# Attention stage of a hybrid block: key projection from mean-free inputs, first batch loaded in four parts, two score-maximum transposes made one

## Chip, cores, metric

The kernel runs on one core of a Trainium2 chip, as one launch. The metric is the device time in microseconds (us) of that core. Before the change three runs gave a median of 1651.34 us (1651.06 to 1651.93).

## What is computed

Eight batches of 512 tokens with 256 features pass through three blocks: a sparse attention with 16 heads of 16 features, a gated linear attention with a feed-forward part, and block-routed feed-forward layers with residuals. Only the first block is touched by the change. Each block is applied to a normalized input. The reference of the attention is

```python
scale = 1.0 / jnp.sqrt(jnp.asarray(DH, dtype=x.dtype))
q = _split_heads(x @ Wq + bq)
k = _split_heads(x @ Wk + bk)
v = _split_heads(x @ Wv + bv)
scores = jnp.einsum('bhqd,bhkd->bhqk', q, k) * scale
sparsity = scores.max(axis=-1) - scores.mean(axis=-1)
_, top_idx = jax.lax.top_k(sparsity, U)          # U = 307 of 512 queries
q_sel = jnp.take_along_axis(q, top_idx[..., None], axis=2)
scores_sel = jnp.einsum('bhud,bhkd->bhuk', q_sel, k) * scale
attn = jax.nn.softmax(scores_sel, axis=-1)
out_sel = jnp.einsum('bhuk,bhkd->bhud', attn, v)
out = jnp.zeros_like(q).at[bi, hi, top_idx].set(out_sel)
return out.transpose(0, 2, 1, 3).reshape(b, l, D) @ Wo + bo
```

If the mean over the keys is taken off every key of a head, the mean of a query's scores is zero. The maximum of the mean-free scores is then the sparsity itself, and the softmax does not change, since each query's scores are shifted by one constant.

## The kernel before

The whole program is one function with SBUF tiles for everything. All matrices are float32. The work on the engines is issued in an order written out in loops; a scheduler then fixes each engine's order, and each engine executes its instructions strictly in that order.

**Loads.** The input of batch 0 (`xres[:, 0]`, 512 KB) is one load on SP's queue (line 48). ACT's queue issues the padded `wq` and `wk` (512 KB each) and `wv` (256 KB, line 77). POOL copies the used columns out of the padded `wq` and `wk` (line 133). SP then issues the bias columns `bq` and `bk`, four small loads each (line 143), the broadcast rows `bo` and `bv` (line 89), and batch 1 (line 162), which is held back until the statistics of batch 0 exist. Batches 2 to 7 are loaded by the same line at later steps.

**Selectors.** `head_of` (POOL, lines 166 to 174) marks the first 16 of each 32 partitions. `own`, `one`, `kept` and `bq_own` (DVE, lines 175 to 187) are made from it and from `ident`. Each of two groups `m` of eight heads fills 128 partitions, 16 for each head, and its q and k are kept in two versions `e` = 0, 1, which hold the even and the odd heads, so that each block of 32 partitions has one head and 16 spare rows.

**front(b)** prepares a batch in pieces (a generator, one piece at each `yield`): DVE (or ACT) normalizes to `xn`; POOL adds `bo` to the residual `xres` (line 286); PE transposes `xn` in two halves (line 295) and ACT copies each to `xnT`, with the sum over the tokens as a by-product (`xsum`, line 298); then for two groups `m` PE projects queries and keys (`q_ps`, `k_ps`, line 316), ACT or DVE write the two versions of q (lines 329, 334), ACT those of k (line 367); then the values (`v_ps`, lines 376 and 385). Between the first q and the first k there is a piece that makes the mean key: eight PE instructions with one column each (`km_ps`, line 344), and four small DVE instructions (lines 350 to 355), which turn it into the bias `kb` of line 367. That bias takes the mean key off each key.

**Steps.** A list of 128 steps (batch, m, e, k) drives the rest. In step n, `max_one` computes four score tiles of 128x512 (PE, line 422) and reduces each to its row maxima (DVE, line 425, to `mx`). Sixteen steps later (`LAG`) `exp_one` computes four transposed score tiles of the older step (PE, line 433), ACT takes the exponential (line 437), and one step after that `weigh` multiplies with the values (PE, line 442). `take` copies the sums out (ACT, line 452), sends a part to `den` (line 454), and POOL puts the halves together (lines 457 to 460). In the first 14 steps (`LEAD`) the pieces of `front(0)` and `front(1)` run between the maxima; later one piece of `front(b + 2)` follows each step. PSUM has three banks for the tag "e" (`bank`), four for "m" (`bank_m`) and one for `acc`; with maxima and exponentials in one step, line 433 uses the first and line 422 the second, and the pieces of `front` also use `bank_m`.

**Placing maxima.** After the last of four steps of a group and version, `place_maxima(b, m, e)` transposes the 16 columns of maxima (PE, line 401), negates them (ACT, line 403) and sends them with eight small DMAs on SP's queue: four into spare rows of the older q (line 406), so that line 433's scores have the maximum taken off, and four into `neg` (line 411). From `neg`, after the last maximum, DVE selects the top queries (lines 467 to 474, 26 rounds), and PE and DVE scale the outputs (lines 617 to 630).

**After the attention** (line 636 on) come the output projection and the other two blocks, which the change leaves as they are.

Of the kernel before, what the change touches and what calls it, by code (L numbers as in the profile page):

```python
# [10 lines left out]
F32 = mybir.dt.float32  # L11
# [27 lines left out]
def block_kernel(ctx: ExitStack, tc: tile.TileContext, t: dict, out: bass.AP):  # L39
# [8 lines left out]
    nc.sync.dma_start(out=xres[:, 0], in_=x_in[:, 0])  # L48

    ident = keep.tile([P, P], F32, name="ident")  # L50
    make_identity(nc, ident)
    eps = keep.tile([P, 1], F32, name="eps")
    nc.gpsimd.memset(eps, LN_EPS)
# [45 lines left out]
    with ExitStack() as outer:  # L99
# [21 lines left out]
        mx = a_out.tile([P, NB, NG, 4 * 4], F32, name="mx")  # L121
# [3 lines left out]
        with ExitStack() as inner:  # L125
# [3 lines left out]

            def load_heads(name, src, eng):  # L130
                wp = load_chunked(a1, name + "_pad", src, eng)
                w = a1.tile([P, NC2, D], F32, name=name)
                nc.gpsimd.tensor_copy(
                    w.rearrange("p c (h d) -> p (c h) d", d=DH),
                    wp.rearrange("p c (h q) -> p (c h) q", q=32)[:, :, 0:DH],
                )
                return w

            def load_head_column(name, src, eng):
                w = a1.tile([P, NC2], F32, name=name)  # L140
                for g in range(NG):
                    r = 64 * (g % 2)
                    eng.dma_start(
                        out=w[r : r + 64, g // 2 : g // 2 + 1],
                        in_=src.rearrange("(j q) g -> j q g", q=32)[:, 0:DH, g : g + 1],
# [13 lines left out]
            def load_after(b, part):  # L159
# [5 lines left out]
            head_of = a1.tile([P, 4], F32, name="head_of")  # L165
            nc.gpsimd.memset(head_of, 1.0)
            nc.gpsimd.affine_select(
                out=head_of, in_=head_of, compare_op=ALU.is_ge, fill=0.0,
                base=0, pattern=[[-32, 4]], channel_multiplier=1,
            )  # L170
            nc.gpsimd.affine_select(
                out=head_of, in_=head_of, compare_op=ALU.is_ge, fill=0.0,
                base=DH - 1, pattern=[[32, 4]], channel_multiplier=-1,
            )
# [11 lines left out]
            for e in range(2):  # L186
                nc.vector.tensor_scalar(bq_own[:, e, :], bq, own[:, e : e + 1], None, ALU.mult)

# [80 lines left out]
            fronts = {}  # L269

            def front(b, pick, alone):
# [3 lines left out]
                for k in range(4):  # L275
# [5 lines left out]
                    else:  # L281
                        nc.vector.tensor_scalar(
                            xn[:, k, :], xres[:, b, k, :], mean, rs, ALU.subtract, ALU.mult
                        )

                nc.gpsimd.tensor_tensor(
                    xres[:, b], xres[:, b],
                    bo.unsqueeze(1).to_broadcast([P, 4, D]), ALU.add,
                )
                xnT = a2.tile([P, NC2, L], F32, tag="xnT", name=f"xnT{b}")  # L290
                xsum = a2.tile([P, NC2], F32, tag="xsum", name=f"xsum{b}")
                for c in range(NC2):
# [7 lines left out]
                    )  # L300
                    yield
# [10 lines left out]
                fronts[b] = (qs, ks, va)  # L312
                kb = a2.tile([P, 2, NC2], F32, tag="kb", name=f"kb{b}")

                def project(ps, w, m, c):
                    nc.tensor.matmul(  # L316
                        ps, w[:, c, bass.ts(m, P)], xnT[:, c, :],
# [3 lines left out]
                for m in range(NC2):  # L321
                    ps = pick(f"q_ps{b}")
                    for c in range(NC2):
                        project(ps, wq, m, c)
# [14 lines left out]
                    if m == 0:  # L339

                        pm = pick(f"km_ps{b}")
                        for mm in range(NC2):
                            for c in range(NC2):
                                nc.tensor.matmul(
                                    pm[:, mm : mm + 1], wk[:, c, bass.ts(mm, P)],
                                    xsum[:, c : c + 1],
                                    start=(c == 0), stop=(c == NC2 - 1),
                                )
                        km = a2.tile([P, NC2], F32, tag="km", name=f"km{b}")
                        nc.vector.scalar_tensor_tensor(  # L350
# [920 lines left out]
```

## Time and profile before

| | |
|---|---|
| median of 3 runs | 1651.34 us |
| profiled execution, its own time | 1653.55 us |
| span of the trace of that execution | 1651.8 us |
| mean granted TensorE clock | 0.988 of full speed |
| busy: PE, DVE, ACT, POOL | 1599.0, 969.4, 671.7, 334.3 us |
| DMA moved | 27.58 MB, mean 17 GB/s |
| line 422 (maxima's scores) / line 433 (exponentials' scores) on PE | 298.9 / 294.3 us busy |
| line 425 (row maxima) on DVE | 329.0 us busy, 684 ns each |
| line 437 (exponentials) on ACT | 276.1 us busy, 599 ns each |

The busy time of an engine is the union of its instructions' spans. PE is shown busy whenever a matmul is under way, so a high share says that it had work, not that the work was as fast as it could be. The trace can also be read as a chain: from the last instruction back to what released each one. An engine that is not on this chain has time to spare at that point.

### The profile page before, as it was taken

To read this page: it belongs to the slowest core of one execution; us is meant where nothing else is said; L and a number is where in the kernel's file an instruction comes from. 1 tells how busy PE (TensorE), PEld (TensorE's weight loads), DVE (VectorE), ACT (ScalarE), POOL (GpSimd) and SP (SyncE) were. 2 spreads that over 40 slices of the span, in tenths; PEclk is the share of its full clock that TensorE was granted. 3 is DMA by queue.
4 is the path that set the end of the run, shared out by engine and by line. 5 is a ranking of instruction groups with operands and counts; after the bars stand their busy time and mean duration, and the time that the engine had idled before them with its cause. 6 is when DMAs were issued, how large, how long until landed. Compare 5 with 4: busy or idle time off the path is not lost.

```text
span 1651.8 us, 19680 instructions
## 1 busy us (share of the span) xinstructions
PE 1599.0 (97%) x7378; PEld 820.1 (50%) x7378; DVE 969.4 (59%) x2015; ACT 671.7 (41%) x1208; POOL 334.3 (20%) x381
## 2 busy tenths in 40 slices
PE   7999999999999969999989999999999999999999
PEld 3323223333233237655564556555555556766666
DVE  6978776676667786447672666277355633344342
ACT  2366666665656814252346123622521352121010
POOL 3111111010000102114342442154223421000000
PEclk9999999999999979999999999999999999999999
DMA  3100000000000051010000001000000010011100
GB/s 109 40 2 3 2 2 3 2 2 3 2 3 3 2 165 26 3 37 13 1 1 0 1 1 27 0 0 1 0 1 1 0 26 1 20 33 35 43 26 26
DMA packets 24276, 27.58 MB, mean 17 GB/s; under 512 B 6229, under 2 KB 20725, under 8 KB 24181
## 3 DMA queue, kind: packets, MB, share of 16 engines
q1 hardware_dynamic: 23108, 24.75, 5.2%
q10 hardware_dynamic: 1072, 1.57, 0.3%
q8 instruction: 58, 0.95, 0.2%
q14 instruction: 38, 0.30, 0.1%
HBM read 21.20 MB, written 4.33 MB: 15 GB/s over the span
## 4 chain that ended last, share of the span: by engine, by line
PE 77%; DVE 14%; ACT 3%; POOL 3%; issue 1%; DMA 1%; SPq 0%; ACTq 0%; POOLq 0%; DVEq 0%
PE y_ps L889 16%; PE h_ps L909 11%; PE s L433 8%; PE s L422 8%; PE swi_ps L936 7%; PE proj_ps L1019 7%; PE av L442 7%; DVE pr L1052 2%; DVE pr L1042 2%; PE ao_ps L775 2%; PE q_ps L316 2%; PE gla_y L1144 2%; DVE mx L425 2%; PE v_ps L376 2%; PE k_ps L316 2%; POOL o L1069 1%
## 5 line engine op out<-in xcount | busy, mean ns | idle before, releaser
L425 DVE TENSOR_REDUCE mx<-s 128x1 f32<-128x512 f32 x512 | 329.0, 684 | 129.8 <-PE s L433 83.0
L437 ACT ACTIVATE e<-s 128x512 f32<-128x512 f32 x512 | 276.1, 599 | 179.0 <-PE s L433 103.5
L422 PE MATMUL s<-k,q 32*128 32x512 f32 x1024 | 298.9, 641 | 3.2 <-ACT k L367 2.5
L433 PE MATMUL s<-q,k 32*128 32x512 f32 x1024 | 294.3, 638 | 0.4 <-DVE mx L425 0.3
L889 PE MATMUL y_ps<-w,h 128*128 128x256 f32 x1024 | 232.9, 383 | 2.9 <-DVE h L918 2.9
L909 PE MATMUL h_ps<-xnT,w 128*128 128x512 f32 x512 | 229.8, 597 | 4.1 <-ACT h L917 4.1
L889 PEld LDWEIGHTS y_ps<-w,h 128*128 128x128 f32 x1024 | 194.1, 192 | 41.0 <-issue 10.8
L909 PEld LDWEIGHTS h_ps<-xnT,w 128*128 128x128 f32 x512 | 95.5, 191 | 113.8 <-issue 107.1
L442 PE MATMUL av<-e,va 128*32 128x512 f32 (+1 forms) x1120 | 141.9, 568 | 3.8 <-ACT e L437 2.4
L918 DVE TENSOR_TENSOR h<-h,mk 128x512 f32<-128x512 f32 x128 | 97.6, 774 | 78.9 <-ACT h L917 70.0
L917 ACT ACTIVATE h<-h_ps,b 128x512 f32<-128x512 f32 x96 | 65.6, 684 | 178.1 <-PE h_ps L909 178.0
L422 PEld LDWEIGHTS s<-k,q 32*128 32x128 f32 x1024 | 89.5, 184 | 86.0 <-DVE mx L425 56.1
L433 PEld LDWEIGHTS s<-q,k 32*128 32x128 f32 x1024 | 88.1, 183 | 80.8 <-ACT e L437 53.8
L894 DVE TENSOR_TENSOR xres<-xres,y_ps 128x512 f32<-128x512 f32 x48 | 32.8, 683 | 162.2 <-PE y_ps L889 125.0
L936 PE MATMUL swi_ps<-zT,w_gate 128*128 128x512 f32 x256 | 122.7, 599 | 4.8 <-DVE h L945 4.8
L936 PE MATMUL swi_ps<-zT,w_up 128*128 128x512 f32 x256 | 121.2, 594 | 0.0
L1019 PE MATMUL proj_ps<-q_w,rT 128*128 128x512 f32 x256 | 118.3, 601 | 0.0
L889 PE MATMUL y_ps<-w_down,h 128*128 128x256 f32 x512 | 116.8, 380 | 0.0
L889 PEld LDWEIGHTS y_ps<-w_down,h 128*128 128x128 f32 x512 | 95.7, 190 | 20.0 <-issue 8.5
L942 ACT ACTIVATE h<-swi_ps 128x512 f32<-128x512 f32 x64 | 38.2, 596 | 156.7 <-PE swi_ps L936 156.6
L1069 POOL TENSOR_TENSOR o<-o,pr 128x512 f32<-128x512 f32 (+2 forms) x56 | 80.9, 1444 | 58.9 <-DVE pr L1052 56.9
L797 POOL TENSOR_TENSOR xres<-xres,b 128x512 f32<-128x512 f32 x32 | 40.1, 1271 | 240.0 <-ACT row L737 217.7
(191 smaller groups left out, 1713.9 us busy)
## 6 DMA issues: line engine op xcount, KB each, us to landing
mk<-md SPq DMA_DIRECT2D x32, 256.0 KB
xres<-in_L_attn_a_x SPq DMA_DIRECT2D x8, 512.0 KB
out<-xres SPq DMA_DIRECT2D x16, 256.0 KB
q<-negT SPq DMA_DIRECT2D x128, 2.0 KB
neg<-negT SPq DMA_DIRECT2D x128, 2.0 KB
w<-in_f_w1T SPq DMA_DIRECT2D x1, 1024.0 KB
w<-in_f_w2T SPq DMA_DIRECT2D x1, 1024.0 KB
w_gate<-in_b_w_gateT SPq DMA_DIRECT2D x1, 1024.0 KB
```

The source lines that it names most:

```text
L316: nc.tensor.matmul(ps, w[:, c, bass.ts(m, P)], xnT[:, c, :], start=(c == 0), stop=(c == NC2 - 1),)
L422: nc.tensor.matmul(s, qs[e][rows, m, bass.ts(k, P)], ks[e][rows, m, :], start=True, stop=True)
L425: nc.vector.tensor_reduce(mx[:, b, 2 * e + m, r : r + 1], s, AX.X, ALU.max)
L433: nc.tensor.matmul(s, ks[e][rows, m, bass.ts(kt, P)], qs[e][rows, m, :], start=True, stop=True)
L437: nc.scalar.activation(ex, s, AF.Exp, scale=1.0 / DH**0.5)
L442: nc.tensor.matmul(av[32 * j : 32 * j + 32, queries], va[:, 8 * kt + 4 * m + j, e, :], es[j][:, queries], start=(kt == 0), stop=(kt == 3 a ...
L889: nc.tensor.matmul(y[0][:, bass.ts(i, D)], h[f][:, bass.ts(2 * u + i, P)], w[:, f, :], start=(f == 0), stop=(f == NF - 1),)
L909: nc.tensor.matmul(ps, w1[:, c, bass.ts(f, P)], xT[g][:, c, :], start=(c == 0), stop=(c == NC2 - 1),)
L918: nc.vector.tensor_tensor(hf, hf, mk[g][:, f, :], ALU.mult)
L936: nc.tensor.matmul(ps, w[:, c, bass.ts(f, P)], zT[g][:, c, :], start=(c == 0), stop=(c == NC2 - 1),)
L1019: nc.tensor.matmul(ps, rT[b // G4][:, c, bass.ts(b % G4, P)], q_w[:, c, m], start=(c == 0), stop=(c == NC2 - 1),)
L1069: nc.gpsimd.tensor_tensor(dst, dst, src, ALU.add)
```

## The change

Parts that only move are cut. The selectors `head_of` now stand ahead of the weight loads on POOL; the tile that takes a padded weight is a buffer of the tag `k1` (three buffers, otherwise the odd keys); `bq` and `bk` come in two loads each instead of four.

```diff
-    nc.sync.dma_start(out=xres[:, 0], in_=x_in[:, 0])
+    for k in range(4):
+        (nc.scalar if k % 2 else nc.sync).dma_start(out=xres[:, 0, k], in_=x_in[:, 0, k])
...
-        mx = a_out.tile([P, NB, NG, 4 * 4], F32, name="mx")
+        mx = a_out.tile([P, NB, NC2, 2, 4 * 4], F32, name="mx")
...
+            def load_heads(name, src, eng):
+                wp = a2.tile([P, NC2, L], F32, tag="k1", name=name + "_pad", bufs=3)
...
+                for r in range(2):
+                    eng.dma_start(
+                        out=w[64 * r : 64 * r + 64, :],
+                        in_=src.rearrange("(j q) g -> j q g", q=32)[:, 0:DH, r::2],
+                    )
...
+            bk_kept = a1.tile([P, 2, NC2], F32, name="bk_kept")
+            nc.gpsimd.tensor_tensor(bk, bk, bk, ALU.subtract)
+            for e in range(2):
+                nc.vector.tensor_scalar(
+                    bk_kept[:, e, :], bk, kept[:, e : e + 1], one[:, e : e + 1],
+                    ALU.mult, ALU.add,
+                )
...
-                nc.gpsimd.tensor_tensor(
-                    xres[:, b], xres[:, b],
-                    bo.unsqueeze(1).to_broadcast([P, 4, D]), ALU.add,
-                )
+                if not alone:
+                    add_bias(b)
                 xnT = a2.tile([P, NC2, L], F32, tag="xnT", name=f"xnT{b}")
+                xcT = a2.tile([P, NC2, L], F32, tag="xcT", name=f"xcT{b}", bufs=1)
...
                     nc.scalar.activation(
                         xnT[:, c, :], ps, AF.Identity, accum_out=xsum[:, c : c + 1]
                     )
+                    mean = xmean[:, c : c + 1]
+                    if b == 0:
+                        nc.vector.tensor_scalar(mean, xsum[:, c : c + 1], -1.0 / L, None, ALU.mult)
+                        nc.vector.tensor_scalar(xcT[:, c, :], ps, mean, None, ALU.add)
+                    else:
+                        nc.scalar.mul(mean, xsum[:, c : c + 1], -1.0 / L)
+                        nc.scalar.activation(xcT[:, c, :], ps, AF.Identity, bias=mean)
                     yield
...
-                    if m == 0:
-                        pm = pick(f"km_ps{b}")
-                        for mm in range(NC2):
-                            for c in range(NC2):
-                                nc.tensor.matmul(
-                                    pm[:, mm : mm + 1], wk[:, c, bass.ts(mm, P)],
-                                    xsum[:, c : c + 1],
...
-                        nc.vector.scalar_tensor_tensor(
-                            km, pm[:, 0:NC2], 1.0 / L, bk, ALU.mult, ALU.add
-                        )
-                        nc.vector.tensor_tensor(km, bk, km, ALU.subtract)
-                        for e in range(2):
-                            nc.vector.tensor_scalar(
-                                kb[:, e, :], km, kept[:, e : e + 1], one[:, e : e + 1],
...
-                        project(ps, wk, m, c)
+                        project(ps, wk, xcT, m, c)
...
-                            bias=kb[:, e, m : m + 1], scale=kept[:, e : e + 1],
+                            bias=bk_kept[:, e, m : m + 1], scale=kept[:, e : e + 1],
...
-            def place_maxima(b, m, e):
+            def place_maxima(b, m, es):
+                n = 16 * len(es)
+                pt = bank_m(f"mxT_ps{b}")[0:n, 0:P]
+                nc.tensor.transpose(
+                    pt, mx[:, b, m].rearrange("p e n -> p (e n)")[:, 16 * es[0] : 16 * es[0] + n],
+                    ident,
+                )
+                negT = a2.tile([32, P], F32, tag="negT", name=f"negT{b}")
+                nc.scalar.mul(negT[0:n, :], pt, -1.0)
...
-            for _ in range(7):
+            for _ in range(6):
                 next(first)
...
-                1: batch_stats([1], None, maximum_of(0)),
+                1: batch_stats([1], lambda: fronts[0][3][0:1, 1, 0:1], maximum_of(0)),
...
                 if ahead is not None and ahead[3] == 3:
-                    full.append((n + 2, ahead[0:3]))
+                    b, m, e = ahead[0:3]
+                    if b == NB - 1 and m == 1:
+                        full.append((n + 2, (b, m, (e,))))
+                    elif e == 1:
+                        full.append((n + 2, (b, m, (0, 1))))
...
+                    if n == 9:
+                        nc.gpsimd.tensor_copy(bo_late[0:1, 0:1], maximum_of(n))
+                        nc.gpsimd.tensor_copy(bo_late, bo)
+                        for b in range(2):
+                            add_bias(b)
...
-                    while done < 23 * (n + 1) // LEAD:
+                    while done < 22 * (n + 1) // LEAD:
```

In words: the token mean is taken off the transposed input itself (`xcT`), and the keys are projected from that instead of from `xnT`. The mean-key piece and its PSUM bank go, and the bias of line 367 becomes a constant. `xcT` is written by DVE for batch 0 and by ACT for the others, from the same PSUM bank as `xnT`. `add_bias` is the addition of `bo` to the residual, from a late copy of `bo`; for batches 0 and 1 it moves to step 9. The statistics of batch 1 wait for `xcT` of batch 0. The maxima of both versions of a group are transposed together after the second; only the last group of the last batch is still done in two halves. The DMAs that place the maxima are as many as before.

## The prediction

> **What bounds the kernel now.** I read busy time by stage first, then the chain of waits from the start to the last maximum, then single microseconds. The stages (from:to, length, busy PE, PEld, DVE, ACT, POOL with counts, granted clock, DMA share, GB/s):
>
> ```profile
> 0.00:19.90 19.90, 8.18 (x24) 4.38 (x24) 8.01 (x38) 4.92 (x11) 7.71 (x23) 1.00 0.47 145
> 19.90:71.10 51.20, 50.26 (x215) 21.28 (x215) 46.51 (x99) 14.96 (x29) 10.36 (x18) 0.97 0.20 63
> 206.00:472.00 266.00, 266.00 (x1728) 82.55 (x1728) 185.16 (x312) 162.87 (x316) 29.54 (x27) 1.00 0.01 3
> 541.00:612.00 71.00, 54.31 (x319) 18.25 (x320) 56.12 (x118) 36.67 (x71) 8.69 (x13) 0.86 0.28 83
> 612.00:1651.80 1039.80, 1019.66 (x3749) 630.74 (x3747) 522.46 (x1178) 325.20 (x545) 255.18 (x263) 0.99 0.05 14
> ```
>
> There are four regimes. Up to 19.9 us no engine is half busy: waits rule. From 19.9 to 71.1 maxima run alone and DVE is busy 46.51 of 51.20. From 71 to 541 exponentials run beside maxima and PE has no gap (266.00 of 266.00 in the middle). From 541 the top queries hold DVE. After 612 come stages that the change does not touch: in the built programs their instructions stand in the same order on every engine, so they can only move as a whole.
>
> The start and two pieces of the middle, as the chain of waits has them (start, length, what), and the rows that hold the start up:
>
> ```profile
> 0.79 5.43 DMA xres<-in_L_attn_a_x
> 8.75 1.26 DVE xn L282 x4
> 10.01 5.46 DMA xres<-in_L_attn_a_x
> 15.49 0.75 DVE ln_st L221 x2
> 19.10 0.79 ACT k L367
> 19.93 1.15 PE s L422 x8
> ...
> 147.38 0.21 PE mxT_ps L401
> ...
> 153.47 0.98 PE km_ps L344 x8
> ```
> ```profile
> 16.84 0.36 DVE L187 TENSOR_SCALAR bq_own<-bq,own 128x2 f32<-128x2 f32 x2
> ...
> 18.71 0.48 DVE L355 TENSOR_SCALAR kb<-km,kept,one 128x2 f32<-128x2 f32 x2
> ```
>
> Batch 0 lands at 6.22, but the chain then runs through batch 1's load (issued 10.01, landed 15.47): DVE's order puts batch 1's statistics ahead of the selectors, of `bq_own` and of the mean-key instructions, so q and k of batch 0 wait for another batch. The first score starts at 19.93.
>
> **The change part by part.**
>
> *(1) Start.* Four loads on two queues put all of batch 0 ahead of `wq`; before, 512 KB of each came together. Four loads from 4 to 7 us ran at 381 to 387 GB/s, and x and `wq` landed at 6.22 and 6.0, so x alone is down about 512 KB / 385 GB/s = 1.4 us earlier, near 4.9. But in the new order ACT issues `wk` only when a part of x is in, and `wv` only when `bq` is, and its table load (1.28) and the root come behind these. I put xn at 8.0 instead of 8.66, transposes done and `xnT` at 10.6 instead of 11.25 and the first q matmul at 10.75 instead of 11.44. q took 11.44 to 14.80, so it ends at 14.1; k follows with its 1.96, ending 16.1 (`xcT` is two DVE pieces of about 0.8, the row of q on line 334, done by 13). Batch 1's load no longer stands behind eight small bias loads but four; SP reaches it near 7, not 10.01, and with its 5.46 it lands by 12.5. Its statistics (DVE 15.49 to 17.75 before, with selectors among them; about 1.9 alone) are over by 15, its root by 15.4. That is before k ends, so k is written at 16.2 to 17.0 and the first score starts at 17.0: 3.0 earlier. Bounds: 1.5, if batch 1 lands at 14.5 and is again last; 4.5, if xn starts 1.4 earlier and k runs at the pace of later k pieces (1.06 each, against 1.96).
>
> The Trainium skill, page "DMA: Bandwidth & Descriptors", section "Issuing engines are not separate DMA queues", says that loads issued by several engines share the same 16 DMA engines and that only issue time is saved. By that rule the second queue would be worth one or two issues of about 0.45, some 0.5 to 1 us here, and this term would be near its lower bound.
>
> *(2) Clock.* Between k (17.4) and the first score PE idled 2.52 us, and then the granted clock fell (columns as above, the clock third from the end; it is back at 24.7):
>
> ```profile
> 21.00:22.00 1.00, 1.00 (x6) 0.45 (x2) 0.83 (x2) 0.00 (x0) 0.16 (x1) 0.55 0.00 0
> 22.00:23.00 1.00, 1.00 (x6) 0.05 (x4) 0.95 (x3) 0.75 (x2) 0.02 (x1) 0.50 0.00 0
> ```
>
> In my sum PE idles 0.9 there. DVE waited 0.86 (24.01 to 24.87) for slow scores, so 0.86 is the most that full clock gives. I take 0.8, lower bound 0.
>
> The skill's page "TensorE: Matmul & The Clock Gate", section "What's actually happening", lets the clock fall after an idle window of about 3.4 us, free-running. The idle gap here was 2.52 us, so by that rule alone there would have been no fall; the row decides.
>
> *(3) Lead, 20 to 71.* DVE loses batch 1's four mean-key instructions: 0.14 + 0.16 + 0.48 = 0.78. PE loses one piece of 0.98, beside DVE's work. Four POOL copies gate batch 1's statistics (0.17 each) during a wait. Adding `bo` to batches 0 and 1 moves to step 9; POOL works there 2.35 us for each, before `spread` and long before `outC` needs it (busy 10.36 of 51.20), and next to maxima at an unchanged 0.6 each. ACT's extra pieces for batch 1 fit (14.96 of 51.20). Gain 0.8, bounds 0 and 1.8 (the piece counts too where two fall in a step).
>
> *(4) Mean-key piece.* Fronts 2 to 7 run beside exponentials, where PE has no gap: 6 x 0.98 = 5.9. Bounds 4.9 (one of the six ends in a wait for something else) and 5.9.
>
> *(5) Transposes of maxima.* 32 become 17. Before, 3 fall in the lead and 29 later; after, 1 and 16. So 13 x 0.21 = 2.7, if a transpose of 32 columns costs as one of 16 (the moved side is 128 wide in both); bounds 2.0 and 2.7. SP issues the same DMAs, 16 in a row instead of 8; at some 0.6 each the older half gets its row four steps later, at step 9 + 2 of a group whose exponentials start at step 16: five steps of 4.1 us spare. The last group is split as before, so the wait from the last maximum to the top queries stays.
>
> *(6) Price on ACT.* Each of 12 transposed halves of fronts 2 to 7 gets a mean (about 0.2, the size of the accumulator row) and an `xcT` (0.60) on ACT, and holds its PSUM bank until then (one such half before, in order of time: start, length, engine and line, the idle time before it in brackets):
>
> ```profile
> 207.07 0.66 PE L295 MATMUL xnT_ps<-ident,xn 128*128 128x128 f32 x4
> 208.17 0.60 ACT L298 ACTIVATE xnT<-xnT_ps 128x512 f32<-128x512 f32 x1
> 208.65 0.21 ACT L298 ACTIVATION_READ_ACCUMULATOR xnT<-xnT_ps 128x1 f32 x1
> 208.82 1.08 ACT L437 ACTIVATE e<-s 128x512 f32<-128x512 f32 x2
> 211.21 1.09 ACT L437 ACTIVATE e<-s 128x512 f32<-128x512 f32 x2 [1.31 <-PE s L433]
> ```
>
> ACT idles 1.31 before the next exponentials, which covers 0.8. But the new ACT order is `xnT`, mean, one exponential, `xcT`, one exponential: mean to 209.1, exponential to 209.65, `xcT` to 210.2. The third score of the next half step, which PE starts at 209.97, takes the bank that `xcT` reads: 0.25 late. That is 12 x 0.25 = 3.0. Bounds: 0, if the four scores in different row groups absorb it; 9.6, if the whole 0.8 shows each time. I take 3.0, the worked row. Queued behind that score are the fourth score, then the next half step; DVE, with 1.3 idle in these steps, follows.
>
> *The sum.* 3.0 + 0.8 + 0.8 + 5.9 + 2.7 - 3.0 = 10.2. Against the profiled span: 1651.8 - 10.2 = 1641.6, and 1643.35 with the 1.75 that lies around it (1653.55). The median of the runs, 1651.34, is 2.2 under that execution, so I predict 1641.1.
>
> **Rivals.** *A, the start gives nothing and ACT takes all.* Term 1 at 1.5, 2 and 3 at 0, 6 at 9.6: 1.5 + 4.9 + 2.7 - 9.6 = -0.5, no change, 1651.8. For it speaks that `xcT` shares a bank with maxima; against it the 1.31 of ACT's idle time.
>
> *B, no price on ACT, and a good start.* 4.5 + 0.86 + 1.8 + 5.9 + 2.7 = 15.8: 1635.5. For it: PE packs four scores, and a late third one may cost nothing.
>
> *C, slower: the held bank.* One place: line 422's third score after each transposed half. If `xcT` there waits for both exponentials of the half step, as `xnT` did when scores came first, the score is late by mean, 1.08 of exponentials and `xcT`: 0.2 + 1.08 + 0.6 less the 0.25 that ACT was ahead, about 1.6. 12 x 1.6 = 19.2 against gains of 13.2: 1657.3. It decides from 13.2 / 12 = 1.1 us a piece. Against it: the built order has only one exponential between.
>
> *D, the change doesn't do what it says at the start:* batch 1's statistics still end last and the score starts at 19.9. Then 0.8 + 5.9 + 2.7 - 3.0 = 6.4: 1644.9. For it: ACT's root for batch 1 still stands before k.
>
> **How the numbers follow.** The forecast, 1641.1 with its own range of 1637 to 1645, gets 0.50; D 0.19, B 0.18, A 0.06, C 0.07. The range leaves out A and C and the end of B: 1635 to 1648, which takes in half of the price bound as well. A measurement of this kernel tells about 0.2%, 3.3 us, from no change. Faster by more: 0.50 + 0.19 + 0.18 = 0.87; same 0.06 (A); slower 0.07 (C).
>
> **What would show it.** The first score at 17 (start right), above 19 (D). The clock at 1.00 from 20 to 25. Period of a batch between transposes: 67.37 before (274.51 to 341.87), 67.37 - 0.98 - 2 x 0.21 = 65.97 without a price, 66.5 with mine, 69 in C, where PE would show idle time on line 432 released by `xcT`. The stage after the last maximum should keep its length of 1111 (540.34 to the end); clock dips in it that fall elsewhere would be outside this sum, and would make it wrong by a few us.

## The result, and the profile after

The changed kernel took 1650.8 us (median of 14 runs, 1648.84 to 1653.82), the kernel before on the same chips 1651.47 (14 runs, 1650.05 to 1652.73). The ratio is 0.9997 with a 95% interval of 0.9989 to 1.0005: no measurable change, where 10 us had been predicted. The profiled execution took 1650.2 us by its own time, with a span of 1648.5 and a mean granted clock of 0.988.

Busy time by stage in the changed kernel (from:to, length, busy PE, PEld, DVE, ACT, POOL with counts, granted clock, DMA share, GB/s), cut where its own first score, first exponentials and last maximum stand:

```profile
0.00:17.77 17.77, 6.95 (x17) 3.41 (x17) 9.24 (x40) 4.96 (x11) 6.12 (x27) 1.00 0.57 163
17.77:69.00 51.23, 50.33 (x213) 21.45 (x215) 47.48 (x98) 18.76 (x36) 13.20 (x21) 1.00 0.20 63
206.00:472.00 266.00, 265.83 (x1680) 81.36 (x1676) 182.62 (x296) 166.79 (x325) 29.49 (x27) 1.00 0.01 3
539.00:610.00 71.00, 56.80 (x323) 19.39 (x324) 55.85 (x118) 36.67 (x71) 8.78 (x13) 0.83 0.27 84
610.00:1648.50 1038.50, 1018.64 (x3746) 630.80 (x3744) 522.35 (x1178) 325.22 (x545) 255.48 (x263) 0.99 0.05 14
```

The start is shorter and the clock of the lead is whole. In the middle PE is as full as before, with 48 fewer matmuls in the same 266 us. 40 of them are matmuls that the change takes out (32 of the mean key, 8 transposes of maxima), and the score matmuls are as many as before, 506 of each kind: less was asked of PE, and it got no further. Four moments in the trace say where the gain went (start times, and the end of the last maximum):

| moment | before | after | difference |
|---|---|---|---|
| first score | 19.93 | 17.77 | -2.16 |
| first score of the exponentials | 69.66 | 65.79 | -3.87 |
| last maximum ends | 541.02 | 538.98 | -2.05 |
| from there to the end | 1110.78 | 1109.52 | -1.26 |

The change gained 3.87 us up to the first exponentials and gave 1.82 back beside them, where it had been expected to gain 5.6. The last row is work that is the same in both kernels; over all the profiled runs below it was between 1106.55 and 1111.48, so 1.26 there says nothing. Part of that spread is the clock, as the prediction warned: after the last maximum the granted clock lacked 13.7 us of full clock in the shortest of these (1106.6), 17.1 in three of 1107.3 to 1107.8 and 22.2 in the two longest (1110.9 and 1111.5). Between the two kernels it does not explain the difference (18.8 before, 20.5 after).

The page's groups of the two score lines in the changed kernel (line, operation, count | busy as a union, mean ns of one | idle time before them and what ended most of it):

```profile
L432 PE MATMUL s<-k,q 32*128 32x512 f32 x1024 | 308.2, 638 | 1.4 <-ACT k L371 0.9
L443 PE MATMUL s<-q,k 32*128 32x512 f32 x1024 | 304.0, 638 | 0.5 <-DVE mx L435 0.3
L443 PEld LDWEIGHTS s<-q,k 32*128 32x128 f32 x1024 | 93.3, 183 | 89.5 <-ACT e L447 61.4
```

and their counterparts in the kernel before:

```profile
L422 PE MATMUL s<-k,q 32*128 32x512 f32 x1024 | 298.9, 641 | 3.2 <-ACT k L367 2.5
L433 PE MATMUL s<-q,k 32*128 32x512 f32 x1024 | 294.3, 638 | 0.4 <-DVE mx L425 0.3
L433 PEld LDWEIGHTS s<-q,k 32*128 32x128 f32 x1024 | 88.1, 183 | 80.8 <-ACT e L437 53.8
```

As many score matmuls, 638 to 641 ns each in both: but the union of their spans grew from 298.9 and 294.3 us to 308.2 and 304.0. Four scores in four row groups run side by side when they start together; the same 1024 matmuls that cover 9 us more time overlap less. The weight loads of the exponentials' scores waited 8.7 us more, 7.6 of it for an exponential. PE's total busy time stayed at 1599.1 us: the work that went out came back as scores that overlap less.

### The profile page after: what moved, and what is told of

It is laid out like the page before. It is cut to its first block, busy times and chain, and to the rows that moved or that the text cites. A ratio compares the mean times of both kernels' runs of the same rounds, so it can differ in the third digit from the quotient of the medians.

```text
span 1648.5 us, 19457 instructions
## 1 busy us (share of the span) xinstructions
PE 1599.1 (97%) x7299; PEld 818.1 (50%) x7299; DVE 966.0 (59%) x1989; ACT 679.6 (41%) x1221; POOL 335.8 (20%) x388
## 4 chain that ended last, share of the span: by engine, by line
PE 71%; DVE 9%; ACT 3%; POOL 3%; issue 1%; DMA 1%; SPq 0%; ACTq 0%; POOLq 0%; DVEq 0%
PE y_ps L908 16%; PE h_ps L928 11%; PE s L443 7%; PE swi_ps L955 7%; PE proj_ps L1038 7%; PE av L452 6%; PE s L432 6%; DVE pr L1071 2%; DVE pr L1061 2%; PE ao_ps L794 2%; PE gla_y L1163 2%; POOL o L1088 2%; PE chT_ps L766 1%; DVE w L1063 1%; DVE h L937 1%
## 5 line engine op out<-in xcount | busy, mean ns | idle before, releaser
L432 PE MATMUL s<-k,q 32*128 32x512 f32 x1024 | 308.2, 638 | 1.4 <-ACT k L371 0.9
L443 PE MATMUL s<-q,k 32*128 32x512 f32 x1024 | 304.0, 638 | 0.5 <-DVE mx L435 0.3
L432 PEld LDWEIGHTS s<-k,q 32*128 32x128 f32 x1024 | 95.2, 183 | 94.2 <-DVE mx L435 67.1
L443 PEld LDWEIGHTS s<-q,k 32*128 32x128 f32 x1024 | 93.3, 183 | 89.5 <-ACT e L447 61.4
```

What stands on the lines that cost most here:

```text
L432: nc.tensor.matmul(s, qs[e][rows, m, bass.ts(k, P)], ks[e][rows, m, :], start=True, stop=True)
L443: nc.tensor.matmul(s, ks[e][rows, m, bass.ts(kt, P)], qs[e][rows, m, :], start=True, stop=True)
```

## What a step costs

Batches 3 to 6 repeat with one period, 67.37 us before and 67.51 after. Cut at each start of the value products, with the piece of `front` that ran in it ("-": none; `mxT`: a transpose of maxima as well), the 16 steps of one period last, in us:

```
before 3.95(xnT) 3.96(xnT) 4.20(q) 4.66(mxT,q) 4.12(km) 4.19(k) 4.19(k) 4.40(mxT,q)
       4.20(q) 4.19(k) 4.19(k) 4.41(mxT,v) 4.20(v) 4.20(v) 4.19(v) 4.11(mxT,-)
after  3.95(xnT) 3.97(xnT) 4.52(q) 4.64(mxT,q) 4.20(k) 4.19(k) 4.22(q) 4.19(q)
       4.19(k) 4.20(k) 4.22(v) 4.65(mxT,v) 4.20(v) 4.19(v) 4.08(-) 3.90(-)
```

Two things stand in it that no busy share shows. A step with nothing in it lasts 3.90 to 4.08, not 4.20 less a piece of 1.06. And a transpose of maxima costs 0.21 beside the first of a pair of projections (4.41 against 4.20) but 0.45 beside the second (4.65). The rows of the changed kernel show both.

A step with no piece (timeline: start, length, engine, line, operation, idle time before it and its releaser):

```profile
402.19 0.69 PE L443 MATMUL s<-q,k 32*128 32x512 f32 x1
...
403.15 0.18 PEld L443 LDWEIGHTS s<-q,k 32*128 32x128 f32 x1 [0.24 <-issue]
...
403.39 1.57 ACT L447 ACTIVATE e<-s 128x512 f32<-128x512 f32 x3 [1.50 <-PE s L443]
...
404.04 0.18 PEld L443 LDWEIGHTS s<-q,k 32*128 32x128 f32 x1 [0.69 <-ACT e L447]
404.04 0.69 PE L443 MATMUL s<-q,k 32*128 32x512 f32 x1
404.04 0.18 PEld L432 LDWEIGHTS s<-k,q 32*128 32x128 f32 x1
...
405.09 1.06 PE L452 MATMUL av<-e,va 128*32 128x512 f32 x8
```

The second half step follows the first at once. Its first two scores start at 403.15, but the next score for the exponentials needs the bank that the first exponential (begun 403.39) still reads, and starts at 404.04, 0.89 late; the maxima's score is issued behind it, so it is just as late. The eight matmuls run as two packs of four instead of one of eight. A piece stands where that wait would be, between one step's second half step and the next step's first, so most of it costs nothing: a step with a projection, 1.06 us of PE, lasts 4.20, only 0.30 more than an empty one of 3.90.

A transpose beside the second half of a pair:

```profile
384.19 1.29 DVE L435 TENSOR_REDUCE mx<-s 128x1 f32<-128x512 f32 x2 [0.89 <-PE s L432]
...
385.06 0.28 PE L405 MATMUL mxT_ps<-ident,mx 128*32 128x128 f32 x1
...
385.28 0.69 PE L432 MATMUL s<-k,q 32*128 32x512 f32 x1
...
385.53 0.18 PEld L432 LDWEIGHTS s<-k,q 32*128 32x128 f32 x1
385.53 0.69 PE L432 MATMUL s<-k,q 32*128 32x512 f32 x1
```

and beside the first of a pair (from the last kernel below, whose step is 4.41):

```profile
309.03 1.29 DVE L439 TENSOR_REDUCE mx<-s 128x1 f32<-128x512 f32 x2 [0.88 <-PE s L436]
...
309.89 0.28 PE L409 MATMUL mxT_ps<-ident,mx 128*32 128x128 f32 x1
...
310.11 0.69 PE L436 MATMUL s<-k,q 32*128 32x512 f32 x1
...
310.12 0.69 PE L436 MATMUL s<-k,q 32*128 32x512 f32 x1
```

Both reductions end 0.42 to 0.43 after the transpose starts (384.19 + 1.29 = 385.48; 309.03 + 1.29 = 310.32). In the second case the two maxima's scores start 0.01 apart and do not wait for it. In the first case the second score starts at 385.53, 0.05 after the reduction ends: with one of the four banks of the tag "m" held by the half-finished projection and one taken by the transpose, the next in turn is the one that DVE is reading. The four banks are in the code. In the trace's records the weight load of the second score waits for DVE's semaphore in both cases; that it is for the bank is read from the code and these times.

## The experiments

Each is one profile and one time beside the kernel before on the same chip, except the last. A single time says little (the 14 runs of the changed kernel spread over 5 us), so the experiments are read by the period and by "steady". "Steady" is the time from the first score of the exponentials to the end of the last maximum: 471.36 in the kernel before, 473.19 in the changed one. It repeats well: two runs below that differ from the changed kernel in the start alone have 473.26 and 473.28.

### Undoing the change part by part

*The dead mean-key piece put back.* Its result is used by nothing.

```diff
+                    if m == 0 and b >= 2:
+                        pm = pick(f"km_ps{b}")
+                        for mm in range(NC2):
+                            for c in range(NC2):
+                                nc.tensor.matmul(
+                                    pm[:, mm : mm + 1], wk[:, c, bass.ts(mm, P)],
+                                    xsum[:, c : c + 1],
+                                    start=(c == 0), stop=(c == NC2 - 1),
+                                )
+                        yield
```

> The changed kernel with the eight one-column matmuls of the mean key put back for batches 2 to 7, as dead work that nobody reads. Theory 'gap': a step without a piece waits 0.7 to 0.85 us for the exponentials that free PSUM banks, so the work fills time that is lost anyway: the batch period (start of the first transposed half to that of the next batch, 67.51 us in the changed kernel) grows by 0.3 us at most, the last maximum ends within 2 us of 538.98. Rival 'work': PE is bound by what it executes, the period grows by 0.98 to 68.5 and the last maximum comes 5.9 us later.

Measured: steady 471.86, period 67.39, span 1646.2, time 1647.91 (before 1652.99). More work on PE, and 1.3 us less. The second transpose of a period falls on the first v piece again (4.42 for 4.65), and a step that was empty (4.08) holds the piece and lasts 4.12.

*The kernel before without the piece.* From batch 2 on its keys take batch 1's mean key off, so the attention of those batches is not the reference's.

```diff
-                kb = a2.tile([P, 2, NC2], F32, tag="kb", name=f"kb{b}")
+                kb = kbs[min(b, 1)]
...
-                    if m == 0:
+                    if m == 0 and b < 2:
```

(`kbs` holds two tiles of the size of `kb`.)

> The kernel before without the mean-key piece for batches 2 to 7 (matmuls and the four DVE instructions are left out; these batches take off batch 1's mean key, so their keys are not mean-free). Theory 'gap': the period falls from 67.37 to 67.1 or 67.25, and the last maximum comes 0.5 to 2 us before 541.03. Rival 'work': the period falls to 66.4, the last maximum comes 5.9 us earlier.

Measured: steady 474.40, 3.04 more than with the piece; period 67.87 (67.37), time 1655.64 (before 1652.99). Neither theory had a loss here. The step lengths say why: in place of `km`'s step of 4.12 the period has an empty one of 4.09 to 4.12 at its end, and all later pieces came a step earlier, which put two more transposes beside second halves (4.64 for 4.40 and 4.41).

*Single transposes.* The changed kernel with 32 of them.

```diff
-                    if b == NB - 1 and m == 1:
-                        full.append((n + 2, (b, m, (e,))))
-                    elif e == 1:
-                        full.append((n + 2, (b, m, (0, 1))))
+                    full.append((n + 2, (b, m, (e,))))
```

> The changed kernel with the maxima of each version transposed by themselves again, 32 transposes instead of 17. Theory 'gap': the shared transpose saves nothing, since 0.21 us twice or 0.45 once is lost either way in the bank rotation: the period stays within 0.2 of 67.51. Rival 'work': two more transposes in a batch, period 67.93, last maximum 2.7 us later.

Measured: steady 476.97, 3.78 more than paired; period 68.19. A transpose takes 0.21 of PE, but two fewer in a batch save 0.68: one of them stood beside a second half. Theory 'gap' failed here: it had the period within 0.2 of 67.51.

*Mean and `xcT` on POOL,* read from `xnT` in SBUF instead of the PSUM bank, from batch 2 on.

```diff
+                    elif b >= 2:
+                        nc.gpsimd.tensor_scalar(mean, xsum[:, c : c + 1], -1.0 / L, None, ALU.mult)
+                        nc.gpsimd.tensor_scalar(xcT[:, c, :], xnT[:, c, :], mean, None, ALU.add)
```

> The changed kernel with mean and xcT of batches 2 to 7 made by POOL from xnT in SBUF, instead of by ACT from the PSUM bank. If the held bank and ACT's two extra instructions cost 0.33 us a batch (the step after the transposes is 4.52 instead of 4.20), the period falls to 67.18 and the last maximum comes 2 us earlier. If the price is elsewhere, nothing changes. If POOL delivers xcT late for the key projection, the period grows.

Measured: steady 470.71, 2.48 less; period 67.22 (the step after the transposed halves 4.20 for 4.52). About 0.95 of the 2.48 is one place, the first exponentials, here in the changed kernel:

```profile
66.62 0.20 ACT L325 ACTIVATE xmean<-xsum 128x1 f32<-128x1 f32 x1
66.85 0.69 ACT L326 ACTIVATE xcT<-xnT_ps,xmean 128x512 f32<-128x512 f32 x1
...
67.56 1.28 ACT L447 ACT_TABLE_LOAD   x1
...
68.85 1.57 ACT L447 ACTIVATE e<-s 128x512 f32<-128x512 f32 x3
```

Mean and `xcT` stand ahead of the table load for the exponentials. From the first score of the exponentials to the next q piece it takes 4.76 us; with the two on POOL, and in the kernel before, 3.80 and 3.81.

The three parts add up: 471.36 + 3.04 (piece out) - 3.78 (paired) + 2.48 (ACT) = 473.10, and 473.19 was measured. The sum goes by the piece's worth in the order of the kernel before; in that of the changed kernel the same piece was worth 1.33 (473.19 - 471.86), so what it is worth depends on what stands beside it.

### What an empty step waits for

*A bank taken without a step:* one dead matmul of one column, in the step of the first k piece.

```diff
+                    if m == 0 and b >= 2:
+                        pm = pick(f"km_ps{b}")
+                        nc.tensor.matmul(
+                            pm[:, 0:1], wk[:, 0, 0:P], xsum[:, 0:1], start=True, stop=True
+                        )
```

> The changed kernel with one dead matmul of one column (about 0.1 us) in place of the mean-key piece for batches 2 to 7: it takes a bank of the ring of four and gives PE nothing to do. Theory 'ring': what the mean-key piece did for the period it did by shifting which instruction gets which bank: the step with a transpose and a value piece falls from 4.65 to 4.42, as with the whole piece put back, and the period is about 67.3 or less. Theory 'gap': only PE work in the gap helps, so the period stays at 67.51 or grows by 0.1.

Measured: period 67.88, steady 477.08, time 1652.88 (before 1652.09). Neither theory had this number. The steps with a transpose stayed at 4.64; of the steps without one, only that with the dead matmul grew, 4.20 to 4.55. So taking one bank out of turn is not what the mean-key piece had done for the transposes; what it had done, the empty step further below shows.

*A later exponential:* 0.2 us of copying on ACT ahead of the first exponential of each half step, in empty steps alone.

```diff
+            tiny = a1.tile([P, 1], F32, name="tiny")
...
+                if j < 2 and 28 <= n < 110 and n % 16 in (12, 13):
+                    nc.scalar.copy(tiny, s[:, 0:1])
```

> The changed kernel with a one-column ACT copy of the score (about 0.2 us) ahead of the first exponential of each half step, in the steps without a piece only. If those steps (4.08 and 3.90) are bound by the exponential that frees the third bank of the ring of three, each grows by 0.2 or more and the period by 0.4 to 0.9. If DVE's maxima or PE bind them, ACT's 1.3 us of idle time in each half step takes the copies and the period stays at 67.51.

Measured: the two empty steps 4.16 and 4.02 (4.08 and 3.90), period 67.70, steady 474.27, time 1649.95 (before 1652.09). The steps grew by less than 0.2 because the exponentials came less than 0.2 late. The second empty step, the counterpart of the one shown above:

```profile
402.51 0.69 PE L444 MATMUL s<-q,k 32*128 32x512 f32 x1
...
403.76 0.16 ACT L448 COPY tiny<-s 128x1 f32<-128x1 f32 x1 [1.55 <-PE s L444]
403.82 1.58 ACT L450 ACTIVATE e<-s 128x512 f32<-128x512 f32 x3
...
404.47 0.69 PE L444 MATMUL s<-q,k 32*128 32x512 f32 x1
```

From the first score to the first exponential it takes 1.31 us (1.20 in the changed kernel), to the next score 1.96 (1.85), and the step lasts 4.02 (3.90). The 0.11 of delay goes through to the score and to the step: an empty step waits for that exponential.

*Something short in the gap:* the value products in two halves, one after each half step, in one of the two empty steps, and from step 110 on.

```diff
-                halves = 96 <= n - LAG - 1 < 112 and (n - LAG - 1) % 4 > 0
+                halves = (n >= 110 or n % 16 in (12, 13)) and 0 < n - LAG - 1 < 112
+                halves = halves and (n - LAG - 1) % 4 > 0
```

> The changed kernel with the value products of one of the two steps without a piece cut in two halves, one behind each half step, as the last steps already have it, and of three more steps after the last piece. Theory 'gap': with 0.5 us of work behind each half step instead of 1.0 behind one, such a step costs 3.5 instead of 3.9 or 4.08: period 67.0 to 67.15, last maximum 2 to 3 us earlier. Rival: no change in the period.

Measured: that step 3.54 (1.79 + 1.75) for 4.08, period 66.98, steady 468.71, time 1647.06 (before 1652.09). No work was taken out; half of the value products now fills the wait.

*The transposes moved:* paired maxima one step later (`n + 3` for `n + 2`).

> The changed kernel with the paired maxima placed one step later (but for the last group). Theory 'step mate', from the step lengths of the runs so far: a transpose of maxima costs 0.21 us in a step with the first piece of a pair of pieces (q, k or v) and 0.45 in a step with the second; removing the mean-key piece moved every later piece by one step and put the transposes beside second pieces. One step later they stand beside first pieces again: both steps at 4.42 instead of 4.65, period 67.05. Theory 'ring' or 'gap' alone: 67.5.

Measured: period 67.19, not 67.05. Beside the first v the transpose cost 0.2 as expected (4.42), but beside the first k 0.33 (4.52), for a reason that no run shows. Time 1651.24 (before 1650.75), and steady 475.01, longer in spite of the shorter period. The clock accounts for this: soon after the first exponentials it fell to one half for some 6.8 us (columns as in the stages above, the clock third from the end):

```profile
71.00:72.00 1.00, 1.00 (x2) 0.00 (x0) 0.93 (x2) 0.53 (x2) 0.00 (x0) 0.58 0.00 0
...
77.00:78.00 1.00, 1.00 (x12) 0.03 (x4) 0.53 (x1) 0.28 (x1) 0.00 (x0) 0.51 0.00 0
```

The microseconds from 71 to 78 lack 3.41 us of full clock; taken off whole, an estimate, steady would be 471.6. No run shows why the clock fell there.

*An empty step* in place of the mean-key piece, and nothing else.

```diff
+                    if m == 0 and b >= 2:
+                        yield
```

> The changed kernel with an empty step where the mean-key piece stood, for batches 2 to 7: no work, but every later piece one step later, as before the change. Theory 'step mate': the value step with the transpose falls from 4.65 to 4.42 and the period to 67.1 or 67.35, below the 67.39 of the run with the dead matmuls. Theory 'gap': without PE work in the step the period stays at 67.5.

Measured: period 67.18 with the second transpose on the first v (4.41) and empty steps of 3.90; steady 470.28, time 1645.99 (before 1650.75). The mean-key piece was worth its place in the order, not its work. This run and the one with the dead piece put back differ by the eight matmuls alone: periods of 67.18 and 67.39, so their own cost is 0.21 a period, not 0.98.

### The start

The changed kernel's start, in its order of time:

```profile
3.60 0.75 DVE L232 BATCH_NORM_STATS2 ln_st<-xres 128x6 f32<-128x256 f32 x2 [2.67 <-DMA xres<-in_L_attn_a_x]
...
5.39 0.14 DVE L174 COPY xres<-ln_mv 1x1 f32<-1x1 f32 x1
...
6.97 0.37 ACTq L78 DMA_DIRECT2D wv<-in_L_attn_a_Wv  x1
...
7.37 1.28 ACT L166 ACT_TABLE_LOAD   x1 [7.37 <-DMA bq<-in_a_bq_pad]
...
8.77 0.28 ACT L236 ACTIVATE ln_rs<-ln_mv,eps 128x4 f32<-128x4 f32 x1
...
9.38 0.73 DVE L301 TENSOR_SCALAR xn<-xres,ln_mv,ln_rs 128x256 f32<-128x256 f32 x2
```

The statistics are done by 5.39, as the smaller loads promised. But ACT does not issue `wv` before 6.97. In the trace's records that issue waits for semaphore 106, which the first load of `bq` signals when it has landed: the loads of the start share eight semaphores, and `wv` is the next on this one. ACT's table load and the root stand behind that issue: `xn` starts at 9.38, later than the 8.66 of the kernel before.

*The root earlier:* `wk`'s load behind ACT's root, `wv`'s on SP.

```diff
+            nc.scalar.activation(root, eps, AF.Sqrt)
             wk = load_heads("wk", t["a_Wk_pad"], nc.scalar)
-            wv = load_chunked(a1, "wv", t["L0_attn_a_Wv"], nc.scalar)
-
-            nc.scalar.activation(root, eps, AF.Sqrt)
...
+            wv = load_chunked(a1, "wv", t["L0_attn_a_Wv"], nc.sync)
```

> The changed kernel with ACT's table load and root issued right behind wq, ahead of wk, and wv on SP's queue behind batch 1. In the changed kernel the statistics of batch 0 are done at 5.35 us, but ACT, which waited at 6.97 for bq before it could issue wv, makes their root at 8.77. If this wait is what ate the earlier landing, the root is made before 7, xn starts 2 us earlier than 9.38, and the first score starts 1 to 2 us before 17.77. If batch 1's load or wk bind, the first score stays within 0.5 of 17.77.

Measured: first score at 19.02, later and not earlier. `xn` did start earlier, at 7.62, but the issue of `wk` now waited for `wq` to land (it had got `wq`'s semaphore, 105), and its columns were copied at 12.84 instead of 8.59: another wait had taken the place of the one removed. Time 1650.02 (before 1652.09). How far a single start can be trusted: in the nine profiles whose start is that of the changed kernel, the first score came at 17.28 to 18.85, and `xn` at 8.61 to 9.93.

*`wv` alone on SP,* with ACT's order else unchanged. The edit stands behind batch 1 in the code; in the trace SP issues `wv` at 7.58, when `wq` has landed and freed its semaphore (7.56), and batch 1 at 8.09.

```diff
-            wv = load_chunked(a1, "wv", t["L0_attn_a_Wv"], nc.scalar)
...
+            wv = load_chunked(a1, "wv", t["L0_attn_a_Wv"], nc.sync)
```

> The changed kernel with wv issued on SP's queue behind batch 1 instead of on ACT's behind wk; the rest of ACT's order stays. ACT then waits for bq no more: the root of batch 0 is made near 5.7 us instead of 8.77, xn starts near 6.3 instead of 9.38, wk lands as before (copied at 8.6). If that wait ate the gain of the four loads, the first score starts 1 to 2.5 us before 17.77; batch 1's statistics, whose load leaves near 7, are the next bound. If it stays at 17.8, another load binds.

Its own start (timeline, as above):

```profile
5.24 0.20 ACT L164 ACTIVATE root<-eps 128x1 f32<-128x1 f32 x1
...
5.95 1.38 DVE L300 TENSOR_SCALAR xn<-xres,ln_mv,ln_rs 128x256 f32<-128x256 f32 x4
...
13.82 0.75 DVE L230 BATCH_NORM_STATS2 ln_st<-xres 128x6 f32<-128x256 f32 x2 [1.36 <-DMA xres<-in_L_attn_a_x]
...
15.61 0.30 ACT L234 ACTIVATE ln_rs<-ln_mv,eps 128x4 f32<-128x4 f32 x1 [2.32 <-DVE ln_mv L231]
15.82 1.43 ACT L370 ACTIVATE k<-k_ps,bk_kept,kept 128x512 f32<-128x512 f32 x2
```

Measured: `xn` at 5.95, 3.4 earlier, but the first score only 1.14 earlier, at 16.63 (0.65 below the earliest of those nine). Now batch 1's load is last: ACT's root for batch 1 stands ahead of k. Time 1646.96 (before 1650.75).

### Together

Four of these edits in one kernel: `wv` on SP; mean and `xcT` on POOL; an empty step from batch 2 on, right after the transposed halves (`yield` ahead of the first q), so that the transposes fall beside first halves (the text below puts that step in the place of the mean key's piece; the edit puts it here); value products in halves in that empty step and from step 110 on.

> The changed kernel with four edits that the earlier runs priced one by one: wv's load issued on SP behind batch 1's (first score 16.6 there); from batch 2 the mean key and its transposed copy on POOL from xnT (period 67.22); from batch 2 an empty step where the mean key's piece stood, so that the paired maxima fall beside first products of a pair (67.18); value products in halves where a step holds only the next xnT and once no pieces are left (66.98). 'Step mate' theory (a step costs by what stands in it with the maxima): the gains of the period add up, 67.51 - 0.29 - 0.33 - 0.3 to 0.5 = 66.4 to 66.6, first score at 16.6, last maximum at 529 to 533, time 1640 to 1644, faster than the kernel before by 0.45 to 0.7%. Rival 'one pool of slack' (the three edits of the steady part take the same slack of the ring, so that only the largest counts): period 66.9 to 67.1, last maximum 534 to 537, time 1644 to 1648.

Measured in five rounds: 1639.83 us (1635.77 to 1640.91), before 1651.72 on the same chip; ratio 0.993, interval 0.9917 to 0.9944. The profile is that of the fastest run, 1635.77. The period is 66.24: 4.41 twice where a transpose stands, 1.64 + 1.89 for the empty step in halves. Steady is 464.11, 9.1 less than in the changed kernel, where the three edits alone had gained 2.5, 2.9 and 4.5: the gains add up, but for 0.8, and are not one slack taken three times. Period, last maximum (527.25) and time all came just below the ranges of that theory. The first score came at 15.12, 1.5 earlier than in the run with `wv` alone; in this execution SP's issue of `bo` took 1.13 us, not 2.39, `wq` landed at 7.05, not 7.56, batch 1 was issued at 7.58, not 8.09, and its statistics began at 12.32, not 13.82. No edit here explains that. The middle, by the same view as at the beginning:

```profile
206.00:472.00 266.00, 266.00 (x1764) 80.20 (x1764) 185.16 (x300) 162.64 (x311) 41.87 (x40) 1.00 0.01 3
```

Against the changed kernel ACT is busy 4.2 us less and POOL 12.4 us more, and PE shows the same 266.00 as in the slower kernel before. The unions of the score matmuls are back at what they were in the kernel before (page, as above):

```profile
L436 PE MATMUL s<-k,q 32*128 32x512 f32 x1024 | 298.4, 638 | 1.7 <-ACT k L375 1.2
L447 PE MATMUL s<-q,k 32*128 32x512 f32 x1024 | 294.5, 639 | 0.4 <-DVE mx L439 0.4
```

## Why the prediction was wrong

Its six terms against what the runs measured:

| step of the prediction | predicted | measured | from |
|---|---|---|---|
| (1) start | 3.0 | 2.16 | first score |
| (2) clock | 0.8 | 1.0 | the run without the piece in the kernel before, where the clock did not fall: first score of the exponentials 68.66, not 69.66 |
| (3) lead | 0.8 | 0.7 | from first score to first exponentials 48.76 in that run, 48.02 in the changed kernel |
| (4) mean-key piece | 5.9 | -3.0 | the same run, steady |
| (5) transposes | 2.7 | 3.8 | single transposes, steady |
| (6) price on ACT | -3.0 | -2.5 | POOL, steady |
| sum | 10.2 | 2.2 | last maximum 2.05 earlier |

**The step that failed is (4):** "Fronts 2 to 7 run beside exponentials, where PE has no gap: 6 x 0.98 = 5.9." PE's busy share of 266.00 in 266.00 was read as capacity in use. It is the union of overlapping spans, and it stays full when scores overlap less: it was 266.00 at a period of 67.37 and again at 66.24. The bounds of this term, 4.9 to 5.9, allowed for one end in a wait; in fact the steps without a piece last 3.90 to 4.16 in the periods of all runs where their value products are whole, so each ends in one. Shown in its place: the eight matmuls themselves cost 0.21 a period, and taking their step out of the order cost 0.33 in the changed kernel (67.51 against 67.18); in the kernel before, the two together made the period 0.50 longer. The evidence lay in the trace of before: its period holds a step with no piece, and that step lasts 4.11 with a transpose in it, where the rule "a step less a piece" gives 4.20 - 1.06 + 0.21 = 3.35. The Trainium skill, page "Perfetto Trace Analysis", section "Identifying the Most-Contended Engine", says that matmul busy share is no good measure of how close PE is to its limit, and points to the share of peak arithmetic and the busy share of weight loads instead. The first half agrees with these runs. Weight loads were busy 82.55, 81.36 and 80.20 of 266 us in the kernel before, the changed and the last one, under a third: they too do not show PE at a limit, but they do not rank the three, since the fastest has the least.

**Nor did it see what the piece's going would move.** Each transpose was priced at 0.21 wherever it fell. Between the 0.98 a period that was expected of (4) and the 0.50 that was lost, 0.97 is the empty step (4.12 became 4.11) and 0.47 the two transposes that came to stand beside second halves. Term 5 was worth more than predicted because pairing took one of these away again.

**(1) was right in mechanism, mis-sized by 0.8** in this execution; the nine executions with this start lie 1.1 to 2.7 earlier than the kernel before's 19.93. Batch 0 landed early and the selectors left the queue of batch 1's statistics, so k was written at 16.94, not 19.10. The waits of ACT's issues that the term named put `xn` at 9.38; the term had 8.0.

**(2), (3) and (6) held.** The granted clock in the microseconds that showed the dip (columns as in the stages above) was whole after PE's idle gap had shrunk to 0.87:

```profile
21.00:22.00 1.00, 0.93 (x6) 0.10 (x2) 1.00 (x3) 1.00 (x3) 0.00 (x0) 1.00 0.52 63
22.00:23.00 1.00, 1.00 (x3) 0.24 (x3) 1.00 (x3) 0.16 (x1) 0.00 (x0) 1.00 1.06 379
```

(6) cost 2.5 for 3.0, but not at 0.25 a piece where the prediction placed it: nearly 1 us falls at the first exponentials, where the prediction counted ACT's pieces as fitting, and about 0.3 in each period after. That the sum came near is partly luck.

**The rivals.** A came nearest by its time (1651.8), but not by its reason: it let ACT take all, and ACT took 2.5. C, the held bank, did not come: the steady part cost 0.14 more a period, not 1.6 a piece. D failed, since the start moved. None of the four doubted (4); that rival was missing, and the range, which went by them, was too narrow by it.

**Left open.** The medians differ by 0.67 and the traces' last maxima by 2.05. The unchanged rest varies by more than the difference between the two, so one profile of each cannot say whether it gave the remaining 1.4 back. That the fourth score of an empty step waits for the exponential is shown by delaying it, and the score behind a transpose waits for DVE by the trace's record; that both wait for a bank is read from the code and from start and end times. No run with a further bank was tried, since all eight are in use.

## What to carry to other kernels

Where small matmuls share PE by row groups, price a removed piece by comparing a step that has it with a step that hasn't, in the trace of before, and not by its own length under a busy share of 100%: what fills a wait costs little (here 0.21 of 0.98 us), and taking it out gains as little. When a piece goes out of an interleaved order, write down which neighbours everything behind it gets. Here the same edits gained 0.7% once an empty step kept the neighbours in place, halved products filled the wait, the new work went to an idle engine and one load's issue had moved to another queue.

## What the runs showed of the hardware

The clock's fall after an idle gap of PE does not go by the gap's length alone. In the lead it fell after gaps of 2.52 us (before) and 1.89 (the run with the earlier root) and did not after 2.18 (`wv` on SP) or 1.45 (the kernel before without the piece). Both falls were of the same size: from the mean granted clock by microseconds, 0.55, 0.50, 0.50, 0.74 in the one and 0.80, 0.50, 0.50, 0.50, 0.99 in the other, each lacks 1.71 us of full clock, which is 3.4 us at one half. In the run with the transposes moved it fell at 71.4, while PE was busy, with no gap over 0.32 us in the 25 us before; that fall lacks 3.41, twice as much. The other stretches of reduced clock in the fourteen traces, those in the later blocks too, lack 1.71 us or a multiple of it, to within 0.03 (one at the very end of a trace left out).

In this program an engine that issues loads can be held by a load that is not its own: ACT issued nothing from 3.98 (the end of `wk`'s issue) to 6.97, when the first of SP's tiny loads of `bq`, issued at 1.71 behind the parts of batch 0, had landed. The cause is the semaphore that both share in this program; which load waits for which follows from the order of all loads on all queues, so each reordering above moved the wait to another load.
